# Adding the last two blocks' results of a routed layer by products with a matrix of ones and zeros, with the order of work laid out anew

## The chip, the cores and the metric

The kernel runs on one core of a Trainium2 chip. The metric is the time of one execution in device microseconds (us); the smaller the better. A profiled execution also leaves a trace, and all views quoted here are views of such a trace: the page of the profile, the chain of work that ended last, the timeline of an engine, and tables by stretches of time. PE is the engine for matrix products, DVE the vector engine, ACT the scalar engine, POOL the GpSimd engine, SP the engine that only issues transfers here.

## The reference, cut to what matters

Two layers, each of cross attention and of a feed-forward part with 8 experts, of which each token takes the best two. All data are float32.

```python
B, S, D = 4, 512, 128          # 4 sequences of 512 tokens, width 128
KV, HEADS, HD = 77, 16, 8      # context of 77 rows per sequence
E, F, TOP_K = 8, 512, 2
for layer in (0, 1):
    x = x + tanh(g_xattn[layer]) * attention(layernorm(x), context)
    xn = layernorm(x)
    w = softmax(xn @ router); keep the best two of 8 for each token
    h = gelu(einsum('td,edf->tef', xn, w1) + b1)
    y = einsum('tef,efd->ted', h, w2) + b2
    x = x + tanh(g_ffn[layer]) * sum over the two kept experts of w * y
```

The attention of layer 1 also has slopes by position and a mask. The output is `x`, of shape (4, 512, 128).

## The kernel before, in words

**Attention** works on one sequence `b` at a time, with tokens in four tiles of 128 (`NT`). `LS`, `LT`, `LU` are the layer norm (statistics on DVE, the power -1/2 on POOL, scaling on ACT, transposes on PE), `Q` the queries, `S0` to `S3` the scores whose row maxima DVE takes, `M` and `W` lower the scores by these maxima, `X0` to `X3` are the exponentials, `U0` to `U3` the weighted sums, `E`, `T`, `N`, `F` divide by the sums, project and add to `x_sb[b]`.

**Routing** (`RS` to `RX`) makes a second layer norm, the logits, the two choices and, by products with a triangle and a matrix of ones, the row of a DRAM table `xg` that each (token, choice) pair goes to. `Z0` to `Z3` send the rows: each `Z` is two indirect DMAs of 128 rows on POOL. Every such DMA has a memset on POOL ahead of it (`Scatters.send`, L416: the memset is L418, the DMA L419). A row carries the token's data, the weight of the pair and, in its last column, the row of a second table `yk` where the result belongs. Sequences 0 and 1 are group 0, sequences 2 and 3 are group 1; each group has its own `xg` and `yk`. When a group's rows are counted (`RB`, `RG`), SP loads 16 numbers, the first row of each block.

**Blocks.** Each group has 16 blocks: 7 of 256 rows and 9 of 128 rows, each of one expert. `w` loads the expert's weights (578 KB, 5 buffers) and `x` the rows (6 buffers), both on SP's queue; `t` transposes on PE and copies on DVE; `u` is the first product with the gelu on ACT; `d` the second product and, on DVE, the bias and the weight of the pair (L681, L687) and the address (L692); `y` sends the results to `yk` with one or two indirect DMAs on POOL (8 buffers `yb`).

**Combine.** `CL` loads a sequence's two results per token from `yk` (two transfers of 256 KB), `CA` adds both to `x_sb[b]` (L718: on POOL in layer 0, on DVE in layer 1) and in layer 1 sends `x_sb[b]` out (L720). A `CL` has to wait until every scatter of its group has landed.

**Order.** Nothing is scheduled by the compiler: `ORDER` is a list of such steps, written out, and every engine and every DMA queue carries out its instructions in that order. A step is written `1d15.1`: layer 1, step `d` of block 15, group 1; for attention and routing steps the last number is the sequence. `hot` is a product of the identity with itself, whose result nobody reads. The last steps of the list before are

```
1t14.1 1CL.0 1u14.1 1t15.1 1y12.1 1d14.1 1CL.1 1y13.1 1u15.1 1y14.1 1d15.1 1CA.0 1CA.1 1y15.1 1CL.2 1CL.3 1CA.2 1CA.3
```

Of the kernel before, what the change touches and what calls it, by code (L numbers as in the profile page):

```python
# [8 lines left out]
F32 = mybir.dt.float32  # L9
# [30 lines left out]
ROWS = SPARE + 2 * CAP  # L40


@with_exitstack
def flamingo_kernel(ctx: ExitStack, tc: tile.TileContext, a: dict, out: bass.AP):
# [15 lines left out]
    def bank():  # L60
        return ps_mm.tile([P, 512], F32, tag="mm", name="mm")
# [36 lines left out]
    def load_mask(b):  # L98
        t = keep.tile([P, NT * KV + S], I32, tag="mi", name="mi", bufs=2)
        nc.sync.dma_start(out=t, in_=a["masks"][b])  # L100
        msk_i[b] = t
# [499 lines left out]
    class Blocks:  # L601


        def __init__(self, routing):
            self.r, self.l, self.group = routing, routing.l, routing.group
            self.w, self.x, self.xT, self.h, self.y = {}, {}, {}, {}, {}
            self.scatters = Scatters()
# [60 lines left out]
        def down(self, i):  # L668
            n, w, h, x = self.size(i), self.w.pop(i), self.h.pop(i), self.x.pop(i)
# [19 lines left out]
            )  # L689

# [3 lines left out]

        def scatter(self, i):
            yb, to = self.y.pop(i)
            for s in range(self.size(i)):
                self.scatters.send(yks[self.l][self.group], yb[:, s, :], to[:, s : s + 1])

    class Combine:  # L700
# [14 lines left out]
        def add(self):  # L715
            x = x_sb[self.b]
            for k in range(2):
                (nc.gpsimd if self.l == 0 else nc.vector).tensor_tensor(x, x, self.y[:, k], ALU.add)  # L718
            if self.l == 1:
                (nc.scalar if self.b == B - 1 else nc.sync).dma_start(out=out[self.b].rearrange("(p t) d -> p t d", p=P), in_=x)  # L720
# [11 lines left out]
    def routing_constants():  # L732
# [25 lines left out]
        return rank, region, below, ones, upper, mark, nth, block_no, row_of, pair_at, spare  # L758
# [3 lines left out]
    fill = const.tile([P, CAP // P * PAY], F32, tag="fill", name="fill")  # L762
# [5 lines left out]
    def clear(g, q):  # L768
        xg = xgs[g]
        for e in range(4 * q, 4 * q + 4, 2):  # L770
            nc.sync.dma_start(
                out=xg[e * REGION : (e + 2) * REGION, :].rearrange("(r q) d -> r (q d)", r=2)[:, : CAP * PAY].rearrange(
                    "r (p f) -> p r f", p=P
                ),
                in_=fill.unsqueeze(1).to_broadcast([P, 2, CAP // P * PAY]),
            )
        if q == 0:
            nc.sync.dma_start(
                out=xg[UNUSED : UNUSED + 256, :].rearrange("(p r) d -> p (r d)", p=P), in_=fill[:, : 2 * PAY]
            )  # L780

# [63 lines left out]
    def part(l, name, n):  # L845
        k, i = name[0], name[1:]
        A, R = at[l][n], routings[l][n // 2]
        if i.isdigit():
            i = int(i)
            if k in "wxtudy":  # L850
                G = blocks[l][n]
                {"w": G.load_w, "x": G.load_x, "t": G.turn, "u": G.up, "d": G.down, "y": G.scatter}[k](i)
# [14 lines left out]
        vclear0 pads0 ldx0 ones0 hot1 ldwv ldctx slots hot2 0LS.0 ldo0 ldgates ldq0 vclear2 gate keys0 vclear1 ldx1  # L867
        ldx2 hot5 ones1 ldx3 0LT.0 0LS.1 ldpos ldmask1 values1 0LS.2 values0 hot0 0LU.0 fill values2 second 0Q.0 0LT.1
        0S3.0 0LT.2 hot4 0S2.0 cleara1 0S0.0 cleara0 0LU.1 ldmask0 0LU.2 0S1.0 mask1 0Q.1 0M.0 0W.0 0S3.1 0Q.2 0LS.3
        0S2.1 0X0.0 0S0.1 0X1.0 0S1.1 pads1 0U0.0 0X2.0 0M.1 0U1.0 0E0.0 clearb0 0W.1 0X3.0 routing 0U2.0 0X0.1 0U3.0  # L870
        0E1.0 0T0.0 0LT.3 0S2.2 0U0.1 0S3.2 0X1.1 0S1.2 0T1.0 0LU.3 0S0.2 0U1.1 0N.0 mask0 0M.2 0X2.1 0E0.1 0F.0 0Q.3
        0X3.1 0RS.0 0W.2 0U2.1 0RT.0 0S3.3 0U3.1 0E1.1 0S2.3 0RU.0 0T0.1 0T1.1 0RL.0 vclear3 0N.1 0RC.0 0RD.0 0X0.2
        0F.1 0RS.1 clearb1 0X1.2 0U0.2 0X2.2 0RM.0 0RN.0 0RX.0 0Z0.0 0RT.1 values3 0S0.3 0U1.2 0S1.3 0M.3 0Z1.0 0RU.1
        0RL.1 mturn0 0W.3 0X3.2 0RC.1 0U2.2 0E0.2 0X0.3 0Z2.0 0Z3.0 0RD.1 0U3.2 0E1.2 0RM.1 0T0.2 0X1.3 0T1.2 0RN.1
        0RX.1 0U0.3 0RB.1 0Z0.1 0N.2 0U1.3 0Z1.1 mturn1 0F.2 0RS.2 0Z2.1 0Z3.1 0X3.3 0X2.3 0RT.2 0RU.2 0RL.2 0RG.1
        0E0.3 0w0.0 0U2.3 0RC.2 0RD.2 0U3.3 0x0.0 0x1.0 0RM.2 0RN.2 0E1.3 0RX.2 0x2.0 0T0.3 0x3.0 0Z0.2 0Z1.2 0x4.0
        0T1.3 0N.3 0t0.0 0F.3 0w1.0 0RS.3 0w2.0 0u0.0 0Z2.2 ldq1 0RT.3 0t1.0 0d0.0 0w3.0 0u1.0 0RU.3 0t2.0 0t3.0 0u2.0
        0w4.0 0d1.0 0t4.0 0RL.3 0u3.0 0RC.3 0w5.0 0Z3.2 0RD.3 0d2.0 0x5.0 0x6.0 0x7.0 0t5.0 0u4.0 0t6.0 0y0.0 0w6.0
        0RM.3 0x8.0 0d3.0 0RN.3 0w7.0 0u5.0 0RX.3 0w8.0 0RB.3 0x9.0 0t7.0 0d4.0 0w9.0 0d5.0 0x10.0 0y1.0 0RG.3 0x11.0
        0u6.0 0t8.0 keys1 0w10.0 0y2.0 0Z0.3 0u7.0 0Z1.3 0t9.0 0d6.0 0w11.0 0u8.0 0Z2.3 0t10.0 0Z3.3 0y3.0 0d7.0 0d8.0  # L880
        0u9.0 hot3 0x12.0 0w12.0 0d9.0 0y4.0 0y5.0 0t11.0 0u10.0 0x13.0 0t12.0 0u11.0 0d10.0 0w13.0 0y6.0 0x14.0
        0w14.0 0x0.1 0w0.1 0t13.0 0u12.0 0d11.0 0x15.0 0w15.0 0x1.1 0u13.0 0t14.0 ldmask2 0y7.0 0d12.0 0t0.1 0u14.0
        0d13.0 0y8.0 0u0.1 0w1.1 0x2.1 0t15.0 0y9.0 0t1.1 0w2.1 0x3.1 0d0.1 0y10.0 0u1.1 0y11.0 0x4.1 0d14.0 0w3.1
        0x5.1 0d1.1 0y12.0 0x6.1 0t2.1 0u15.0 0y13.0 0t3.1 0d15.0 0w4.1 0x7.1 0w5.1 0y14.0 0y15.0 0u2.1 0w6.1 0u3.1
        0t4.1 0y0.1 0d2.1 0t5.1 0u4.1 0y1.1 ldmask3 0w7.1 0t6.1 0d3.1 0u5.1 0CL.0 0t7.1 0CA.0 0d4.1 0d5.1 0u6.1 0x8.1
        0u7.1 0CL.1 0w8.1 0CA.1 0x9.1 1LS.0 0w9.1 0t8.1 0w10.1 0d6.1 0u8.1 0t9.1 1LT.0 0y2.1 0x10.1 0d7.1 1LS.1 0w11.1
        0d8.1 0x11.1 0t10.1 0y3.1 1LU.0 0w12.1 0y4.1 0u9.1 ldo1 1Q.0 0y5.1 0t11.1 1S0.0 0y6.1 0u10.1 1LT.1 0w13.1
        0d9.1 0x12.1 0t12.1 1S2.0 0u11.1 0d10.1 1S1.0 1LU.1 0u12.1 0y7.1 0w14.1 0d11.1 0x13.1 1S3.0 1M.0 1Q.1 0y8.1
        0t13.1 1S0.1 0u13.1 0y9.1 0x14.1 0w15.1 0t14.1 0x15.1 0d12.1 0t15.1 1S2.1 0u14.1 1W.0 1S1.1 0d13.1 0u15.1
        0y10.1 0y11.1 1X0.0 0y12.1 0d14.1 0y13.1 0y14.1 0d15.1 1S3.1 0y15.1 1U0.0 1M.1 0CL.2 1X1.0 1X2.0 1U1.0 1W.1  # L890
        1X3.0 1E0.0 1U2.0 0CL.3 mask2 0CA.2 1X0.1 1LS.2 1U3.0 1E1.0 1X1.1 1LT.2 1U0.1 1T0.0 1X2.1 mturn2 1T1.0 1U1.1
        1LU.2 0CA.3 1LS.3 1N.0 1X3.1 1F.0 1Q.2 mask3 1RS.0 1S0.2 1RT.0 mturn3 1U2.1 1E0.1 1LT.3 1S2.2 1S1.2 1U3.1
        1S3.2 1E1.1 1RU.0 1LU.3 1M.2 1T0.1 1T1.1 1RL.0 1W.2 1N.1 1RC.0 1RD.0 1X1.2 1F.1 1X0.2 1Q.3 1RM.0 1RN.0 1RS.1
        1RX.0 1Z0.0 1RT.1 1S0.3 1U0.2 1S3.3 1RU.1 1X2.2 1RL.1 1RC.1 1Z1.0 1S2.3 1U1.2 1RD.1 1Z2.0 1X3.2 1U2.2 1RM.1
        1S1.3 1E0.2 1RN.1 1Z3.0 1U3.2 1E1.2 1RX.1 1Z0.1 1M.3 1T0.2 1T1.2 1W.3 1N.2 1X0.3 1RB.1 1F.2 1X1.3 1U0.3 1Z1.1
        1X2.3 1Z2.1 1Z3.1 1RG.1 1U1.3 1X3.3 1U2.3 1U3.3 1E0.3 1RS.2 1w0.0 1w1.0 1E1.3 1x0.0 1RT.2 1T0.3 1x1.0 1T1.3
        1N.3 1RU.2 1F.3 1t0.0 1RL.2 1u0.0 1w2.0 1RC.2 1RS.3 1RD.2 1x2.0 1x3.0 1d0.0 1t1.0 1w3.0 1y0.0 1RT.3 1w4.0
        1RM.2 1RN.2 1RX.2 1u1.0 1t2.0 1RU.3 1t3.0 1x4.0 1x5.0 1x6.0 1RL.3 1u2.0 1RC.3 1RD.3 1Z0.2 1RM.3 1t4.0 1d1.0
        1RN.3 1w5.0 1x7.0 1Z1.2 1u3.0 1w6.0 1RX.3 1t5.0 1Z2.2 1RB.3 1d2.0 1d3.0 1u4.0 1Z3.2 1x8.0 1Z0.3 1Z1.3 1Z2.3
        1x9.0 1RG.3 1d4.0 1u5.0 1d5.0 1w7.0 1t6.0 1t7.0 1u6.0 1t8.0 1w8.0 1u7.0 1w9.0 1w0.1 1Z3.3 1y1.0 1x0.1 1d6.0  # L900
        1d7.0 1u8.0 1t9.0 1u9.0 1y2.0 1y3.0 1y4.0 1x1.1 1x10.0 1d8.0 1w10.0 1x2.1 1t0.1 1t1.1 1u0.1 1w1.1 1t10.0 1y5.0
        1d0.1 1w2.1 1d9.0 1y6.0 1x3.1 1x4.1 1w3.1 1u10.0 1t2.1 1y7.0 1x11.0 1u1.1 1d1.1 1y0.1 1t3.1 1u2.1 1x5.1 1d10.0
# [100 lines left out]
```

## Time and profile before

| | us |
|---|---|
| median of 3 runs (427.59 to 429.42) | 428.34 |
| the profiled execution, its own time | 429.68 |
| its span in the trace | 427.6 |
| PE busy | 385.3 (90%) |
| POOL busy | 295.5 (69%) |
| DVE busy | 244.9 (57%) |
| ACT busy | 225.0 (53%) |

The span runs from the first to the last event of the trace; the execution's own time holds 2.1 us more. PE is the busiest engine over the whole span, but a mean says little here: attention, blocks and the end have different limits.

### The profile page before, as it was taken

To read this page: it belongs to the slowest core of one execution; us is meant where nothing else is said; L and a number is where in the kernel's file an instruction comes from. 1 tells how busy PE (TensorE), PEld (TensorE's weight loads), DVE (VectorE), ACT (ScalarE), POOL (GpSimd) and SP (SyncE) were. 2 spreads that over 40 slices of the span, in tenths; PEclk is the share of its full clock that TensorE was granted. 3 is DMA by queue.
4 is the path that set the end of the run, shared out by engine and by line. 5 is a ranking of instruction groups with operands and counts; after the bars stand their busy time and mean duration, and the time that the engine had idled before them with its cause. 6 is when DMAs were issued, how large, how long until landed. Compare 5 with 4: busy or idle time off the path is not lost.

```text
span 427.6 us, 9653 instructions
## 1 busy us (share of the span) xinstructions
PE 385.3 (90%) x3236; PEld 271.4 (63%) x3236; DVE 244.9 (57%) x931; ACT 225.0 (53%) x529; POOL 295.5 (69%) x478
## 2 busy tenths in 40 slices
PE   5999999987899999989999999999889999999850
PEld 2454545433789999987772355442669789988840
DVE  7786768864447634376774379684648233333342
ACT  2556776663374654447455965446564344435430
POOL 4743312887698989869986450987289898989860
PEclk9999999996699999999999999999989999999995
DMA  7396091112956799986514221014743776789855
GB/s 191 158 372 202 3 325 72 33 44 83 317 150 207 224 361 295 313 299 218 167 45 151 80 60 62 26 45 122 236 129 105 272 232 192 266 285 289 269 204 182
DMA packets 38977, 77.91 MB, mean 182 GB/s; under 512 B 6224, under 2 KB 22608, under 8 KB 38928
## 3 DMA queue, kind: packets, MB, share of 16 engines
q1 hardware_dynamic: 32640, 65.66, 47.9%
q0 software_dynamic: 4992, 10.30, 6.7%
q10 hardware_dynamic: 1296, 1.34, 0.9%
q8 instruction: 26, 0.43, 0.4%
q14 instruction: 23, 0.19, 0.1%
HBM read 55.47 MB, written 21.80 MB: 181 GB/s over the span
## 4 chain that ended last, share of the span: by engine, by line
PE 68%; DVE 12%; DMA 6%; POOL 5%; ACT 4%; issue 3%; SPq 0%; DVEq 0%; ACTq 0%; POOLq 0%
PE mm L673 16%; PE mm L658 15%; PE mm L353 8%; PE o L367 7%; PE mm L305 6%; POOL xg L419 3%; PE mm L279 3%; DVE mx L313 2%; PE mm L347 2%; ACT eT L359 2%; POOL apart L418 2%; PE mm L241 2%; PE mm L643 2%; PE mm L406 2%; DMA xb<-xg 1%
## 5 line engine op out<-in xcount | busy, mean ns | idle before, releaser
L664 ACT ACTIVATE h<-mm,w 128x128 f32<-128x128 f32 (+1 forms) x256 | 86.7, 415 | 99.3 <-issue 55.9
L419 POOL DMA_INDIRECT yk<-yb,to x92 | 89.6, 974 | 18.5 <-issue 12.2
L658 PE MATMUL mm<-xbT,w 128*128 128x128 f32 (+1 forms) x512 | 95.0, 331 | 6.6 <-DVE xbT L645 5.5
L673 PE MATMUL mm<-w,h 128*128 128x128 f32 x736 | 96.0, 281 | 0.7 <-ACT h L664 0.4
L673 PEld LDWEIGHTS mm<-w,h 128*128 128x128 f32 x736 | 89.2, 191 | 6.5 <-ACT h L664 3.6
L658 PEld LDWEIGHTS mm<-xbT,w 128*128 128x128 f32 x512 | 77.1, 194 | 15.0 <-DVE xbT L645 7.7
L418 POOL MEMSET apart<- 1x512 f32 x156 | 80.2, 514 | 0.1
L359 ACT ACTIVATE eT<-mm 77x512 f32<-77x512 f32 x128 | 65.4, 592 | 26.2 <-PE mm L353 25.7
L419 POOL DMA_INDIRECT xg<-rows,rows_to x64 | 62.8, 981 | 15.2 <-issue 13.0
L681 DVE TENSOR_TENSOR yb<-mm,w 128x128 f32<-128x128 f32 (+1 forms) x64 | 22.3, 348 | 67.2 <-PE mm L673 58.6
L313 DVE TENSOR_REDUCE mx<-mm 128x4 f32<-128x308 f32 x128 | 52.1, 469 | 11.5 <-PE mm L305 11.3
L353 PE MATMUL mm<-qa,kb 32*77 32x512 f32 x256 | 41.3, 617 | 0.5 <-DVE mx L313 0.5
L222 POOL TENSOR_SCALAR rstd<-mv 128x4 f32<-128x4 f32 x16 | 3.8, 236 | 54.2 <-DVE mv L220 40.9
L645 DVE COPY xbT<-mm 128x128 f32<-128x128 f32 (+1 forms) x64 | 21.7, 344 | 30.4 <-PE mm L643 30.4
L367 PE MATMUL o<-eT,vb 128*32 128x512 f32 x256 | 36.6, 631 | 0.0
L305 PE MATMUL mm<-kb,q 32*128 32x154 f32 x512 | 31.8, 322 | 0.8 <-DVE mx L313 0.5
L305 PEld LDWEIGHTS mm<-kb,q 32*128 32x128 f32 x512 | 22.6, 183 | 12.4 <-issue 3.1
L687 DVE TENSOR_TENSOR yb<-yb,xb 128x128 f32<-128x128 f32 (+1 forms) x64 | 24.1, 376 | 2.2
L643 PE MATMUL mm<-ident,xb 128*128 128x128 f32 x92 | 20.5, 281 | 1.2 <-DMA xb<-xg 1.2
L353 PEld LDWEIGHTS mm<-qa,kb 32*77 32x77 f32 x256 | 10.5, 140 | 13.4 <-issue 5.6
L223 POOL TENSOR_TENSOR rstd<-rstd,mhalf 128x4 f32<-128x4 f32 x16 | 16.7, 1044 | 1.3
L219 DVE BATCH_NORM_STATS2 st<-x 128x6 f32<-128x128 f32 x64 | 17.1, 267 | 0.2
(155 smaller groups left out, 445.6 us busy)
## 6 DMA issues: line engine op xcount, KB each, us to landing
w<-in_experts SPq DMA_DIRECT2D x64, 578.0 KB, 5.0
xg<-fill SPq DMA_DIRECT2D x8, 1040.0 KB, 6.0
xb<-xg SPq DMA_DIRECT2D x28, 130.0 KB, 3.6
y<-yk SPq DMA_DIRECT2D x14, 256.0 KB, 3.9
mt<-turns SPq DMA_DIRECT2D x4, 820.0 KB
xb<-xg SPq DMA_DIRECT2D x36, 65.0 KB, 4.4
mi<-in_masks SPq DMA_DIRECT2D x4, 410.0 KB
turns<-mb SPq DMA_DIRECT2D x8, 205.0 KB
```

Source lines behind the costliest of these rows:

```text
L305: nc.tensor.matmul(view[g][:, h], lhsT=self.q[h][rows, t * P : (t + 1) * P], rhs=kbs[l][rows, h, :, b, :], start=(l == 0), stop=(l == 0 or ...
L313: nc.vector.tensor_reduce(self.mx[:, t, :, 2 * g : 2 * g + 2], view[g], AX.X, ALU.max)
L353: nc.tensor.matmul(ps[g][:KV, :], lhsT=kbs[l][rows, h, w, b, :], rhs=self.qa[h][rows, :], start=(l == 0), stop=True,)
L359: nc.scalar.activation(self.eT[j][g][:KV, :], ps[g][:KV, :], AF.Exp)
L367: nc.tensor.matmul(self.o[a][g * 32 : (g + 1) * 32, :], lhsT=vbs[self.b][:, self.l, g, j, :], rhs=self.eT[j][g], start=(w == 0), stop=(w = ...
L418: nc.gpsimd.memset(apart, 0.0)
L419: i = nc.gpsimd.indirect_dma_start(out=to[:, :], out_offset=bass.IndirectOffsetOnAxis(ap=index, axis=0), in_=rows, in_offset=None)
L643: nc.tensor.transpose(ps[:, s * P : (s + 1) * P], x[:, s, :D], ident)
L658: nc.tensor.matmul(ps[:, g * 256 : g * 256 + n], lhsT=w[:, c * P : (c + 1) * P], rhs=xT[:, :n], start=True, stop=True,)
L664: nc.scalar.activation(h[:, c, :n], ps[:, g * 256 : g * 256 + n], AF.Gelu_apprx_tanh, bias=w[:, B1_AT + c : B1_AT + c + 1])
L673: nc.tensor.matmul(y[:, s * P : (s + 1) * P], lhsT=h[:, c, s * P : (s + 1) * P], rhs=w[:, W2_AT + c * P : W2_AT + (c + 1) * P], start=(c = ...
L687: nc.vector.tensor_tensor(yb[:, :n, :], yb[:, :n, :], x[:, :n, D : D + 1].to_broadcast([P, n, D]), ALU.mult)
```

## The change

The results of blocks 14 and 15 of layer 1, group 1, no longer go to `yk`. For each of these blocks a new step `o` (`match`) compares on DVE the token number of each row with all 1024 tokens of the group, which gives a matrix of ones and zeros `oh` (128 x 2 x 512); `y` of these blocks (`give`) multiplies `oh` with the block's results on PE (8 products of 128x128x128) and adds the two outputs of 128x512 to `x_sb[2]` and `x_sb[3]` on DVE. The output of sequences 2 and 3 is sent by block 15's `give`, no more by `CA`. Rows of `yk` that now stay unwritten are cleared once (`cleary`, one transfer of 1 MB). To make room, the buffer of zeros `fill` becomes a quarter wide enough for four rows a partition, `clear` issues four transfers instead of two for the same bytes, and the raw masks have one buffer instead of two. `ORDER` is laid out anew from end to end.

```diff
-        t = keep.tile([P, NT * KV + S], I32, tag="mi", name="mi", bufs=2)
+        t = keep.tile([P, NT * KV + S], I32, tag="mi", name="mi", bufs=1)
...
+            if self.last(i):
+                self.y[i] = yb, None
+                return
...
+        def last(self, i):
+            return self.l == 1 and self.group == 1 and i >= NBLK - LAST
+
+        def match(self, i):
+
+            v = self.x[i][:, 0, D + 1 : D + 2]
+            tok = small.tile([P, 2], F32, tag="tok", name="tok", bufs=2)
+            nc.vector.tensor_scalar(tok[:, 0:1], v, float(ROWS + SPARE + CAP), -float(CAP), ALU.is_ge, ALU.mult)
+            nc.vector.tensor_tensor(tok[:, 0:1], tok[:, 0:1], v, ALU.add)
+            nc.vector.tensor_scalar(tok[:, 1:2], tok[:, 0:1], -float(S), None, ALU.add)
+            oh = blk.tile([P, 2, S], F32, tag="oh", name="oh", bufs=1)
+            for b in range(2):
+                nc.vector.tensor_scalar(oh[:, b], token_at, tok[:, b : b + 1], None, ALU.is_equal)
+            self.oh[i] = oh
+
+        def give(self, i):
+
+            yb, _ = self.y.pop(i)
+            oh = self.oh.pop(i)
+            for b in range(2):
+                ps = bank()
+                for t in range(NT):
+                    own = slice(t * P, (t + 1) * P)
+                    nc.tensor.matmul(ps[:, own], lhsT=oh[:, b, own], rhs=yb[:, 0, :], start=True, stop=True)
+                x = x_sb[2 + b]
+                nc.vector.tensor_tensor(x, x, ps.rearrange("p (t d) -> p t d", d=D), ALU.add)
+                if i == NBLK - 1:
+                    (nc.scalar if b else nc.sync).dma_start(out=out[2 + b].rearrange("(p t) d -> p t d", p=P), in_=x)
+
         def scatter(self, i):
+            if self.last(i):
+                self.give(i)
+                return
...
-            if self.l == 1:
-                (nc.scalar if self.b == B - 1 else nc.sync).dma_start(out=out[self.b].rearrange("(p t) d -> p t d", p=P), in_=x)
+            if self.l == 1 and self.b < 2:
+                nc.sync.dma_start(out=out[self.b].rearrange("(p t) d -> p t d", p=P), in_=x)
...
+        token_at = counted("token_at", [P, S], [[1, NT], [NT, P]], base=ROWS + SPARE)
...
-    fill = const.tile([P, CAP // P * PAY], F32, tag="fill", name="fill")
+    fill = const.tile([P, 4 * PAY], F32, tag="fill", name="fill")
...
-        for e in range(4 * q, 4 * q + 4, 2):
+        for e in range(4 * q, 4 * q + 4):
...
+    def clear_results():
+
+        nc.sync.dma_start(
+            out=yks[1][1][ROWS + SPARE :, :].rearrange("(n p r) d -> p n (r d)", r=4, p=P),
+            in_=fill[:, : 4 * D].unsqueeze(1).to_broadcast([P, 2 * CAP // 512, 4 * D]),
+        )
```

Of the order, these stretches are spoken of below. The kernel's first steps, layer 0 at the first blocks, layer 1 at the first blocks, and the end, each before (-) and after (+), with steps between them left out where "..." stands:

```diff
- vclear0 pads0 ldx0 ones0 hot1 ldwv ldctx slots hot2 0LS.0 ldo0 ldgates ldq0
+ ones0 ldctx vclear2 hot2 ldx0 pads0 slots hot1 ldgates ldwv ldq0 vclear0 0LS.0
...
- 0RX.2 0x2.0 0T0.3 0x3.0 0Z0.2 0Z1.2 0x4.0 0T1.3 0N.3 0t0.0 0F.3 0w1.0 0RS.3
+ 0T0.3 0w1.0 0RN.2 0RX.2 0E1.3 0x3.0 0T1.3 hot3 0N.3 0Z0.2 0w2.0 0F.3 0x4.0 mturn0 0t0.0 0t1.0 0Z1.2 0u0.0 0t2.0 0Z2.2 0x5.0 0RS.3
...
- 1Z2.1 1Z3.1 1RG.1 ... 1RS.2 ... 1t0.0 1RL.2 1u0.0 1w2.0 1RC.2 1RS.3 1RD.2 ... 1d0.0 1t1.0 1w3.0 1y0.0 1RT.3 1w4.0 1RM.2 1RN.2 1RX.2 ... 1Z0.2
+ 1Z2.1 1RS.2 ... 1Z3.1 1RG.1 1RT.2 ... 1RL.2 ... 1RC.2 1RD.2 1RM.2 1x4.0 1F.3 1RN.2 1RX.2 1t0.0 1x5.0 1Z0.2 ... 1RS.3 ... 1u0.0 ... 1Z3.2 ... 1y0.0
...
+ 1y15.0 1t13.1 1w13.1 1y7.1 1u12.1 1x14.1 1w14.1 1CL.0 1x15.1 1o14.1 1u13.1 1y8.1 1d12.1
+ 1t14.1 1y9.1 1w15.1 1d13.1 1y10.1 1u14.1 1CL.1 1CA.0 1y11.1 1t15.1 1y12.1 1d14.1 1u15.1 1CA.1 1d15.1 1y13.1
+ 1CL.2 1y14.1 1CL.3 1o15.1 1CA.2 1CA.3 1y15.1
```

## The prediction, on record before the changed kernel ran

> **What bounds the kernel now.** First the page, slices of 10.7 us:
>
> ```profile
> PE   5999999987899999989999999999889999999850
> POOL 4743312887698989869986450987289898989860
> PEclk9999999996699999999999999999989999999995
> ```
>
> PE is close to full except at the start, around slice 9, around slice 28 and at the end. POOL is as full in the two stretches of blocks (slices 10 to 20 and 29 to 38). Of what ended the span I read the chain of waits from 400 us on; columns are start, length, what:
>
> ```profile
> 412.30 1.28 PE mm L673 x8
> ...
> 417.85 4.21 DMA y<-yk
> ...
> 423.48 0.69 DVE x L718
> ```
>
> After PE's last product (413.58) 14 us pass without PE: the last scatter, its landing, the load back, the adds, the output. The scatters before it are in POOL's timeline (start, length, what, in brackets the idle time before and what ended it):
>
> ```profile
> 402.86 0.96 POOL L419 DMA_INDIRECT yk<-yb,to  x1 [0.17 <-DVE yb L681]
> ...
> 409.44 0.96 POOL L419 DMA_INDIRECT yk<-yb,to  x1 [0.17 <-issue]
> ...
> 412.35 0.96 POOL L419 DMA_INDIRECT yk<-yb,to  x1 [1.44 <-DVE to L692]
> ...
> 414.56 1.16 POOL L419 DMA_INDIRECT yk<-yb,to  x1 [0.73 <-DVE to L692]
> ```
>
> The first is `1y15.0`; six scatters follow it. Four of them lie (409.44 - 402.86) / 4 = 1.645 us apart with 0.17 us of idle time: POOL is saturated there, and has been since 311.40 us, where layer 1's first scatter stands. So the end is set by POOL's queue, and I count from T0, the start of `1y15.0`'s scatter. Before, the end is T0 + 24.7.
>
> Last, PE at layer 0's first blocks and the granted clock there (PE's and four more busy times, PEclk, DMA share, GB/s):
>
> ```profile
> 108.00:112.00 4.00, 2.82 (x12) 2.45 (x13) 1.12 (x4) 1.87 (x2) 3.60 (x5) 0.55 0.96 264
> 112.00:116.00 4.00, 4.00 (x16) 3.36 (x16) 2.31 (x9) 1.03 (x3) 2.35 (x5) 0.60 0.99 354
> ```
>
> A pause of 1.43 us before `0N.3` (108.88) was followed by about 6.5 us at half clock.
>
> **The end, counted from T0.** The change leaves seven scatters behind `1y15.0` (`1y7.1` to `1y13.1`) instead of six, and `1CL.2` waits for the last.
> - Seven at 1.645 and the last one's 0.96: POOL is done at T0 + 12.5.
> - Landing: unknown, since the last scatter now lands while weights and `CL.1` are loaded. Bounds: 1.4 us (415.72 to the load's issue at 417.11, nothing else in flight) and 4.1 us (`1y15.0` ended at 403.82, `1CL.0` was issued at 407.96, DMA busy). I take the middle, 2.75, because part of the traffic is over by then: T0 + 15.2.
> - Loads of `CL.2` and `CL.3`: 417.47 to 422.06, 4.6: T0 + 19.8.
> - `CA.2` and `CA.3`, four adds of 0.69: T0 + 22.6. The two adds of `1y15.1` read PSUM; the nearest row is L408, 128x512 from PSUM, 0.75 each: T0 + 24.1.
> - From the last add to the end as before, 424.17 to 427.6: T0 + 27.5.
>
> [...]
>
> The other path to the same adds goes by block 15. SP's queue now holds `x15` and `w15` behind `CL.0`, which waits for `1y15.0` to land. `CL.0` is issued at T0 + 5.1, as before; two issues of it 0.9, `x15` 0.6, `w15` 0.3: T0 + 6.9. `w15` lands 5.1 later (the chain has a `w` of 5.06): T0 + 12.0. From `u15` to the end of `d15` 2.4 us (411.18 to 413.58): T0 + 14.4. `1y14.1`: 8 products, 16 rows at 0.11 (L673, 8 in 0.89): T0 + 16.2, one add 0.75: T0 + 17.0. `1o15.1`: three small operations at 0.16 and two of 128x512, between 0.24 (L801, 128x32) and 0.75 (L408); I take 0.75, the row of that width: 2.0, so T0 + 19.0. That is 0.8 us ahead of the loads: block 15, the products and the comparisons hide behind the loads, and cost what exceeds 0.8 us. `1y15.1`'s products, at half clock after PE's pause (the clock fell to 0.50 from 416 us on), take 3.5 us and lie beside `CA.2` and `CA.3` and the first add, 3.5 us.
>
> So the end after T0 is 2.8 us **longer** than before; what pays is that T0 is earlier.
>
> **T0.** Before it stand three scatters fewer than before (the two lists, counted): 3 x 1.645 = 4.9 us earlier while POOL is saturated. `d15.0` permits it: it stands 5.8 us of PE work earlier in the new list, and before it was ready at 399.9, 3 us ahead of its scatter.
>
> Upstream, four terms:
> - Start: `wk` was issued at 4.17, after `wv` had landed (the chain has 0.80 + 3.35), the transfers having eight slots. In the new list it is the seventh transfer and issues about 1.4 us earlier. ACT's norm of sequence 0 (11.77) stands behind the four `kb` that need `wk`, and needs `nmr` (10.99; 0.3 earlier, one operation of 0.3 less on the way): it can start at about 10.7. Taken: -1.1.
> - `values3` now stands ahead of `0RX.0`: four copies of 0.15, +0.6 on POOL's first `Z`.
> - `0T0.3` stands ahead of `0RX.2`: 0.36 + 0.42 on DVE, +0.8.
> - `0RS.3` made POOL wait 1.40 us at 115.39; it now stands two scatters later: -1.4.
>
> Sum -1.1. `hot3` moves from the middle of the blocks (0.9 us of PE) into the pause before `0N.3`. If the clock then stays up, PE gains up to 2.1 us at 115, but at 153 to 159 the chain goes through POOL and a landing (`yk`, 5.21 us), and PE would wait there. I take 0 and keep -2.1 for the range.
>
> Layer 1: `1RS.2` stands ahead of `1Z3.1`, and `1RX.2` ahead of `1t0.0`. The first scatter after the pause, `1Z0.2`, can start at about 308.2 (`1U3.3` ends at 299.2, then some 2.8 us to the logits' end at 302, then 5.7 us from logits to `rows_to`, as from 101.58 to 107.29 in layer 0) instead of `1y0.0` at 311.40; but 1.3 us of `1RS.3` no longer lies in the pause. Gain 0 to 1.9; PE waits for `1RN.2` before its first block, so I take 1.0.
>
> T0 = 402.86 - 4.9 - 1.1 - 1.0 = 395.9, and the span ends at 395.9 + 27.5 = 423.4, 4.2 us earlier. The profiled execution's own 429.68 becomes 425.5. The runs' median lies 1.34 below it, so I predict 428.34 - 4.2 = 424.1.
>
> **Edits costed at nothing.** `clear`: eight more issues on SP at 0.86, 6.9 us; SP stood 24.2 us waiting for the masks in those 55 us, and `xg` is first written at 75.1. If the cover failed, the first `Z` would slip by up to 6.9. `cleary`: one issue and 1 MB, 2.6 us at the 390 GB/s of full stretches; it stands at layer 0's blocks where the DMA share is 0.34 to 0.87, and the `w` behind it slip by that much within five buffers; uncovered, 2.6. One mask buffer: `ldmask3` waits for POOL's `mask2`, and `ldo1` and `x` of layer 1 stand near it on SP; needed only by `1S0.3`; uncovered about 3 (`mask` took 3.0). The early `wk1`/`wq1` and `x3` behind `turns1`: `x3` should land near 32.5 and is read at about 36; the margin is 3.5 us, and what exceeds it stops DVE's maxima. `token_at`: between 0.2 (iota 128x32) and 0.95 (memset 128x1024) on POOL, in 6.95 us of idle time before `0RS.0`. `1CA.0` and `1CA.1` (1.4 each on DVE) now stand ahead of `t15`'s copy and `d15`'s bias; they lie beside the wait for `w15`.
>
> **Rivals.**
> 1. *Given back at the end* (0.20). `w15` lands 3 us later, since 512 KB of `CL.0` and two `xb` go ahead of it (one `xb` took 5.61 us in this stretch). Then block 15 decides: T0 + 29.6, and with T0 at 397 a span of 426.6, 427.3 by the median. For it: DMA share 0.9 there. Against: the weights of block 15 were never late before.
> 2. *Slower: PE starved at layer 1's first block* (0.17). `1RN.2` now stands ahead of `1t0.0` on PE, so PE waits out the choice of experts: 5.7 + 0.7 + 0.4 us, then half clock for 6.6 us (3.3 lost), 10.1 in all against some 4 lost there now (1.4 and 0.6 of waits, clock 0.65 in 312 to 316). Everything in POOL's queue follows: T0 = 395.9 + 1.0 + 6.1 = 403.0, span 430.5, 431.2 by the median. It decides from T0 = 402.2 on. Against: `1N.3` and `1F.3`, some 2 us of PE work, stand inside that wait.
> 3. *More than forecast* (0.13). The clock stays up at 108 to 116, POOL starts 1.9 earlier and the landing takes 1.4: T0 = 392.9, span 419.0, 419.7 by the median.
>
> **How the numbers follow.** The forecast has 0.50; its own range, from the bounds above, is 419.7 to 427.5. About 0.5% (2.1 us) is what a measurement of this kernel can tell from no change: 426.2 and 430.5. Faster takes forecast and rival 3 without a little of the upper end, 0.62; same, mostly rival 1, 0.21; slower 0.17. For 8 in 10 the range goes from 417.5 to 431.0.
>
> **What would show it.** `1y15.0`'s scatter near 396 and the last scatter seven places behind it; SP's `CL.2` some 2.75 us after that one's end; DVE's last four `x` adds and two PSUM adds back to back behind the load; layer 0's clock at 108 to 116. I am wrong if `1y15.0` stands later than 402, if DVE's last adds wait for PE and not for the load, or if POOL shows pauses over 2 us between 310 and 395.

## The result, and the profile after

The changed kernel takes 427.27 us by the median of 20 runs (425.4 to 430.33), the kernel before 430.38 by 20 runs beside it. The ratio of the two is 0.9947, with a 95% interval of 0.9926 to 0.9968: faster by 0.5%, some 2.3 us. (The ratio leaves disturbed executions of both out, the medians do not.) The forecast was 424.1 us, 4.2 us faster. The sign and the range held; the size was too large.

The two profiled executions lie apart by just the forecast: 425.46 us (span 423.7) against 429.68 (427.6). That agreement is luck, as the steps show. (0.3 us of the 4.2 lie outside the span: in every run of the changed kernel its own time holds 1.7 to 1.8 us more than its span, before about 2.1. No run tells why.) First the page, slices of 10.6 us:

```profile
PE   6899999987899989999999999989899688999992
POOL 5443251898789889869886540996199898989750
PEclk9999999996999999999999999989799999999999
```

Counted from 1: PE now has a hollow at slices 32 to 34 (328 to 360 us), where it was full before. The clock has new dips at slices 27 and 29 beside the one at slice 10; the dips of before at 11, 30 and 40 are gone. The end, in the chain of waits (start, length, what):

```profile
400.91 5.30 DMA y<-yk
...
406.85 0.96 POOL yk L420
...
408.50 3.41 DMA yk<-yb,to
...
412.30 4.24 DMA y<-yk
...
417.96 0.69 DVE x L754
```

The last scatter starts at 408.50 (1.24 us long) instead of 414.56; its landing is over at 411.90, 2.2 us after its end, and the loads behind it end at 416.54. POOL's timeline from `1y15.0`, whose start is T0:

```profile
394.55 0.96 POOL L420 DMA_INDIRECT yk<-yb,to  x1 [0.17 <-issue]
396.19 0.96 POOL L420 DMA_INDIRECT yk<-yb,to  x1 [0.17 <-issue]
397.84 0.96 POOL L420 DMA_INDIRECT yk<-yb,to  x1 [0.17 <-issue]
400.71 0.96 POOL L420 DMA_INDIRECT yk<-yb,to  x1 [1.40 <-DVE to L696]
402.36 0.97 POOL L420 DMA_INDIRECT yk<-yb,to  x1 [0.17 <-issue]
404.01 1.08 POOL L420 DMA_INDIRECT yk<-yb,to  x1 [0.17 <-DVE tok L707]
406.85 0.96 POOL L420 DMA_INDIRECT yk<-yb,to  x1 [1.24 <-DVE xbT L646]
408.50 1.24 POOL L420 DMA_INDIRECT yk<-yb,to  x1 [0.17 <-issue]
```

Seven scatters follow T0, as said, but two of them stand behind pauses of 1.40 and 1.24 us: POOL is no longer saturated there. The names in the brackets are DVE's steps of a block, and these stand behind PE's products: POOL waits for PE. The addresses (`to`) of block 12, before and after, show that PE is no earlier at this block than before:

```profile
406.19 0.15 DVE L692 TENSOR_TENSOR to<-xb,spare 128x1 int32<-128x1 f32 x1
```

```profile
406.42 0.15 DVE L696 TENSOR_TENSOR to<-xb,spare 128x1 int32<-128x1 f32 x1
```

They are ready at 406.34 and 406.57. Last, layer 0's first blocks (PE and four more busy times, PEclk, DMA share, GB/s):

```profile
108.00:112.00 4.00, 2.29 (x17) 1.84 (x17) 1.30 (x4) 1.87 (x2) 3.66 (x6) 1.00 0.95 274
112.00:116.00 4.00, 4.00 (x21) 3.54 (x22) 1.92 (x9) 2.60 (x7) 3.49 (x6) 1.00 1.00 315
```

The clock is 1.00 where it was 0.55 and 0.60.

### The profile page after: what moved, and what is told of

The parts are those of the page before. It is cut to its first block, busy times and chain, and to the rows that moved or that the text cites. A ratio compares the mean times of both kernels' runs of the same rounds, so it can differ in the third digit from the quotient of the medians.

```text
span 423.7 us, 9735 instructions
## 1 busy us (share of the span) xinstructions
PE 386.9 (91%) x3268; PEld 274.4 (65%) x3268; DVE 248.6 (59%) x943; ACT 225.1 (53%) x529; POOL 294.2 (69%) x475
## 4 chain that ended last, share of the span: by engine, by line
PE 54%; POOL 17%; DMA 11%; DVE 7%; issue 6%; ACT 3%; DVEq 0%; SPq 0%; POOLq 0%; ACTq 0%
PE mm L659 10%; PE mm L674 10%; POOL xg L420 9%; PE mm L354 7%; PE o L368 6%; PE mm L306 6%; POOL apart L419 5%; PE mm L280 3%; DMA xg<-rows,rows_to 2%; DMA w<-in_experts 2%; DMA y<-yk 2%; DMA yk<-yb,to 2%; PE mm L242 2%; POOL yk L420 2%; PE mm L348 2%
## 5 line engine op out<-in xcount | busy, mean ns | idle before, releaser
L659 PE MATMUL mm<-xbT,w 128*128 128x128 f32 (+1 forms) x512 | 93.8, 328 | 9.1 <-DMA w<-in_experts 5.6
L420 POOL DMA_INDIRECT yk<-yb,to x90 | 87.9, 976 | 17.5 <-issue 12.9
L674 PE MATMUL mm<-w,h 128*128 128x128 f32 x736 | 94.6, 279 | 0.5 <-ACT h L665 0.2
L360 ACT ACTIVATE eT<-mm 77x512 f32<-77x512 f32 x128 | 65.5, 592 | 27.5 <-PE mm L354 27.1
L419 POOL MEMSET apart<- 1x512 f32 x154 | 79.2, 514 | 0.1
L354 PE MATMUL mm<-qa,kb 32*77 32x512 f32 x256 | 42.4, 623 | 0.1
L688 DVE TENSOR_TENSOR yb<-yb,xb 128x128 f32<-128x128 f32 (+1 forms) x64 | 22.5, 352 | 2.2
```

The lines of the kernel that those rows point to most:

```text
L354: nc.tensor.matmul(ps[g][:KV, :], lhsT=kbs[l][rows, h, w, b, :], rhs=self.qa[h][rows, :], start=(l == 0), stop=True,)
L360: nc.scalar.activation(self.eT[j][g][:KV, :], ps[g][:KV, :], AF.Exp)
L419: nc.gpsimd.memset(apart, 0.0)
L420: i = nc.gpsimd.indirect_dma_start(out=to[:, :], out_offset=bass.IndirectOffsetOnAxis(ap=index, axis=0), in_=rows, in_offset=None)
L659: nc.tensor.matmul(ps[:, g * 256 : g * 256 + n], lhsT=w[:, c * P : (c + 1) * P], rhs=xT[:, :n], start=True, stop=True,)
L674: nc.tensor.matmul(y[:, s * P : (s + 1) * P], lhsT=h[:, c, s * P : (s + 1) * P], rhs=w[:, W2_AT + c * P : W2_AT + (c + 1) * P], start=(c = ...
```

## The experiments: the two halves of the change

Ratios are to the kernel before on the same chip, with 95% intervals. First the changed kernel again, then each half alone.

> The changed kernel once more, unaltered, for a second profiled execution and for its place beside the parts that run on the same chip. Theory A (the gain is real and about as large as between the medians: -3 us): ratio to before 0.992 to 0.995, and the second profile shows the last scatter of y13.1 near 408.5 to 410 and the same two pauses of POOL (1.2 and 1.1 us) before it. Rival B (the first profile was an early one, and its T0 of 394.55 is not typical): in the second profile 1y15.0 starts 1.5 to 2 us later, at 396 to 396.5, with the steps behind it unchanged, and the execution takes about 427.3.

Measured: 0.9955 (0.9921 to 0.999), median 427.66 against 429.77. The second profile has span 424.6, T0 at 394.73, the two pauses again and the last scatter at 409.06. Theory A holds; T0 is not what was untypical.

```diff
# e2: the order of before, with
+ 0d5.0 cleary
- 1t14.1 1CL.0 1u14.1 1t15.1 1y12.1 1d14.1 1CL.1 1y13.1 1u15.1 1y14.1 1d15.1 1CA.0 1CA.1 1y15.1 1CL.2 1CL.3 1CA.2 1CA.3
+ 1t14.1 1CL.0 1o14.1 1u14.1 1t15.1 1y12.1 1d14.1 1CL.1 1CA.0 1u15.1 1CA.1 1d15.1 1y13.1 1CL.2 1y14.1 1CL.3 1o15.1 1CA.2 1CA.3 1y15.1
```

> The order of before, with the last two blocks' results given by products (clear of the rows, comparisons, products, outputs behind them); only ldmask0 and ldmask3 are moved behind mask1 and mask2, for the one mask buffer. Theory A (end and order add up, some half each): y13.1's scatter stays at 409.4, CL.2 is issued some 2.5 us after its end, 412.9, loads until 417.5, four adds to 420.3, two adds from PSUM to 422, end 425.5: 2.1 us faster, ratio 0.993 to 0.997. Rival B (the end gives all of it): ratio 0.990 to 0.993, the order alone 1.000. Rival C (the end gives nothing, since comparisons and products replace the landing): ratio 0.998 to 1.002.

(`ldmask0` and `ldmask3` moved besides, as said there.) Measured: 1.0005 (0.996 to 1.005). The end alone gives nothing that can be measured: rival C by its number, though not by its reason. The last scatter starts at 410.55, 4 us earlier than before, but the chain of waits of this kernel shows what came then:

```profile
415.96 0.15 SPq L756
...
416.66 4.19 DMA y<-yk
...
422.27 0.69 DVE x L754
```

That scatter ended at 411.52. The other half of these loads, on ACT, was issued at 415.78, so the landing took 4.3 us; on SP they stood behind the output of sequence 1 (L756) to 416.28. In these microseconds `CL.0` and `CL.1` are loaded, 1 MB issued at 409.44 to 411.21.

```diff
# e3: the order of the changed kernel, with
- LAST = 2
+ LAST = 0
- 1d15.1 1y13.1 1CL.2 1y14.1 1CL.3 1o15.1 1CA.2 1CA.3 1y15.1
+ 1d15.1 1y13.1 1y14.1 1y15.1 1CL.2 1CL.3 1CA.2 1CA.3
```

> The order of the changed kernel, with LAST = 0: blocks 14 and 15 are scattered again behind y13.1, no comparisons, no products, no clear of the result rows. Theory A: POOL's saturated stretch in layer 1 starts some 3.4 us earlier as in the changed kernel, T0 at 394.5 to 396, but d15 ends only at about 411.5, so the last scatter stands near 412.3 (before 414.56) and the end follows 12 us behind its end as before: 425 to 425.5, 2.3 us faster, ratio 0.993 to 0.997. Rival B (order gives nothing): ratio 0.999 to 1.001. Rival C (order gives all of it): 0.990 to 0.993.

(The `o` steps and `cleary` are left out too, and `CA` sends all four outputs again.) Measured: 0.9974 (0.9942 to 1.0006). T0 stands at 395.03, as expected, but the last scatter starts at 415.65, not 412.3, 1.1 us later than before the change, and the wait ahead of it (1.66 us) is for DVE's `to` of block 15. With 7.8 us gained at T0, POOL's queue was empty before PE had block 15. So each half removes one of two limits: the order alone leaves the last scatters waiting for PE, the end alone leaves the landing behind the loads of `CL.0` and `CL.1`. The intervals are too wide to show by times alone that the halves together give more than their sum; the traces show the two limits.

## The experiments: the end

```diff
# e5: 1y15.0 behind 1y9.1; both e5 and e6:
- 1CL.0 1x15.1 ... 1w15.1
+ 1x15.1 ... 1w15.1 1CL.0
```

> The changed kernel with 1y15.0 three places later in POOL's queue (behind 1y9.1, six products' scatters... the place that it has before the change: four scatters of this list behind it), and CL.0 behind w15.1 on SP. Theory A (the end pays only because 1y15.0 stands early: CL.0 and CL.1, 1 MB, are then loaded before y13.1 lands; in the run of the end alone they were issued at 409.4 to 411.2 and y13.1's landing took 4.3 us where the changed kernel shows 2.2): CL.0 is issued at about 405, the landing of y13.1 takes 3.5 to 4.5 us, CL.2 is issued about 2 us later, and the kernel is 1.5 to 2.5 us slower than the changed one. Rival B (the landing does not depend on these loads): the landing stays at 2.2 to 2.5 us and the time within 0.7 us of the changed kernel's.

> The changed kernel with CL.0's two loads behind x15 and w15 on SP's queue, nothing else. Theory A (SP waits for a buffer of w there anyway, and block 15 has slack): x15 and w15 are issued about 1 us earlier, POOL's pauses before y9.1 and y12.1 stay within 0.3 us, time within 0.7 us of the changed kernel. Rival B (rival 1 of the prediction: the loads of CL.0 hold block 15 and through it the end): the end comes 1 us or more earlier.

Measured on one chip: e5 1.0006 (0.9971 to 1.0041), e6 0.9966 (0.9929 to 1.0003); medians 430.33 and 428.86. In e5 `CL.0` was issued only at 408.65, later than expected, and the landing of `1y13.1` took 3.7 us (its scatter ended at 411.76, ACT's loads were issued at 415.50); in e6 2.7 us (end 412.07, ACT's loads at 414.72). The direction is theory A's; 1.5 us between the medians is at its lower edge, and the intervals overlap. In e6 nothing was won, but the edit moved little: `w15` was issued at T0 + 7.5 instead of T0 + 7.7, because SP waited for a buffer there anyway. `CL.0` ahead of `x15` and `w15` thus costs next to nothing, and rival 1's mechanism is not what took the rest.

## The experiments: layer 1's first blocks

```diff
# e9
- 1F.3 1RN.2 1RX.2 1t0.0 ... 1u0.0
+ 1F.3 1t0.0 1u0.0 1RN.2 1RX.2
```

> The changed kernel with 1t0.0 and 1u0.0 ahead of 1RN.2 on PE, as they stand before the change: the place of rival 2. Theory A (layer 1's first scatters wait for the choice of experts, and PE's pause there costs nothing that POOL does not lose anyway): 1Z0.2 starts 0.5 to 2.5 us later than 306.4, because 1.8 us of u0 or a wait for its weights stand before the places; the end is 0 to 2 us later. Rival B (rival 2, PE starved there, is where part of the forecast was lost): granted clock stays up in 302 to 309 and the kernel is 1 to 2 us faster than the changed one.

Measured: 1.0081 (1.0051 to 1.011), the largest effect of all: some 5 us slower than the changed kernel, beyond what theory A allowed (1Z0.2 was to slip by 2.5 us at most). PE waits in `u0` for its input, with the places of sequence 2 (L522) behind it; then POOL's first scatter after the pause. Two views of e9, PE's timeline and POOL's:

```profile
306.43 1.99 PE L659 MATMUL mm<-xbT,w 128*128 128x256 f32 x8 [2.25 <-DVE xbT L646]
308.26 0.30 PE L522 MATMUL mm<-m,upper 128*128 128x32 f32 x2
```

```profile
310.30 0.98 POOL L420 DMA_INDIRECT xg<-rows,rows_to  x1 [10.07 <-issue]
```

In the changed kernel that scatter stands at 306.51. The 3.8 us are found again at T0 (398.42) and at the last scatter (412.31): a late start of layer 1 reaches the end undiminished (with both pauses of POOL again, 1.27 and 1.25 us, so PE is late by as much). So rival 2's place is where the new order gains; the change from `1t0.0` to `1RN.2` ahead is a cause of the gain, not a loss.

Where PE loses its lead, the waits of the changed kernel between 332 and 362 us tell (us in total, times, longest). Two of SP's between 300 and 350 tell what stood ahead of the loads:

```profile
PE mm L659 <- DMA w<-in_experts: 5.3, 2, 3.3
PE mm L644 <- DMA xb<-xg: 1.5, 1, 1.5
PE mm L659 <- DVE xbT L646: 0.2, 1, 0.2
```

```profile
SPq L597 <- DVE begins L596: 8.6, 1, 8.6
...
SPq L632 <- DMA xg<-rows,rows_to: 5.7, 1, 5.7
```

Before the change PE waited 2.1 us in the same stretch, and not for `w`. Two kernels were meant to win this back.

```diff
# e7
- 1w0.1 1u7.0 ... 1Z3.3 1x0.1 1u8.0 1y1.0 1t0.1 1d8.0 1t9.0 1y2.0 1x1.1 1x10.0 1u0.1 1u9.0 1d0.1 1w1.1 1t10.0 1x11.0 1w10.0
+ 1u7.0 ... 1w9.0 1w0.1 ... 1Z3.3 1x10.0 1w10.0 1u8.0 1y1.0 1x11.0 1x0.1 1d8.0 1t9.0 1y2.0 1u9.0 1t10.0 1t0.1 1d9.0 1x1.1 1u0.1 1u10.0 1d0.1 1w1.1
# e17
- w = blk.tile([P, WROW], F32, tag="w", name="w", bufs=5)
+ w = blk.tile([P, WROW], F32, tag="w", name="w", bufs=6)
```

> The changed kernel with 1x0.1 (which waits for the landing of Z3.3) and 1w0.1 later on SP, so that x10, w10 and x11 of group 0 go ahead of that wait, and 1t0.1, 1u0.1 behind u9 and t10 on PE. Theory A (PE's lead is lost between 332 and 360, where it waits 3.3 us for w, 1.5 for xb, 2.0 for w, and SP stands 6 us at x0.1; that lead is what POOL waits for before y9.1 and y12.1): PE's waits for loads in 332 to 360 fall from 6.8 to about 3 us, the two pauses of POOL (1.2 and 1.1) shrink below 0.5, y13.1 stands 1.5 to 2.3 us earlier and the kernel is 1.5 to 2 us faster than the changed one. Rival B (there the transfers themselves are the bound, and the order on SP only shifts who waits): PE's waits keep their sum within 1 us, and the time stays within 0.7 us.

> The changed kernel with six buffers of expert weights instead of five (room for it comes from scaling the output bias in place); the order is untouched. Theory A (the term of the forecast that failed is POOL saturated to its end: PE comes late to d9 and d12 because it stood 6.8 us at loads between 332 and 360, 5.3 of it at w, whose issue waits for a buffer): PE's waits for w there fall below 2.5 us, the scatters from 1y7.1 to 1y13.1 take 11 to 12 us instead of 12.3, the kernel is 1.5 to 2.5 us faster than the changed one, ratio to before 0.988 to 0.991. Rival B (the transfers themselves or the landing of Z3.3 hold PE): waits for w within 1.5 us of 5.3, ratio 0.993 to 0.996.

Measured: e7 0.9919 (0.9889 to 0.9949), e17 0.993 (0.9899 to 0.9961). In e7 PE's waits in 332 to 362 sum to 6.6 us instead of 7.0: only the names changed, although the last scatter stands 1.1 us earlier (407.42) and the time is perhaps 0.3% better. In e17 the waits for `w` there are as long as in the changed kernel:

```profile
PE mm L659 <- DMA w<-in_experts: 5.6, 2, 3.4
```

For the first and longer wait both theories named the wrong holder. Neither a buffer nor `x0.1` keeps `w7` of group 0 back, but L597, ahead of both on SP: `1RG.3`, the reading of group 1's block table into SP's registers, stands in the order ahead of `1w7.0`, waits 8.6 us for `begins`, and only then are the next four loads of weights issued (333.04 to 336.55). That is read from the trace; a kernel with `1RG.3` behind `1w9.0` was not run. The second wait (2.0 us, at 358) is not a wait for `w` any more in e7, but waits for rows (`xb`, and `xbT` made from them) stand in its place.

## The experiments: the clock

> The changed kernel with hot3 back at its old place behind 0u9.0, so that nothing runs on PE in the pause before 0N.3. Theory A (the clock falls again but POOL sets the time there): clock 0.5 to 0.6 at 108 to 116, PE some 2 us later at 0t0.0, and 0y0.0's scatter the same to 0.5 us later because POOL is saturated from 0Z0.2 on; time against the changed kernel 0 to +0.5 us. Rival B: the 1.4 us that POOL gains between 0Z0.2 and 0Z0.3 come from the clock, and the kernel is 1.5 us slower than the changed one.

Measured: 0.9961 (0.9925 to 0.9996), as the changed kernel. The pause before `0N.3` was 1.47 us long with nothing in it, and the clock stayed up all the same; windows of e4:

```profile
108.00:112.00 4.00, 2.38 (x17) 1.94 (x18) 1.30 (x4) 1.87 (x2) 3.66 (x6) 1.00 0.96 260
112.00:116.00 4.00, 3.73 (x18) 3.08 (x19) 1.88 (x10) 2.22 (x6) 3.49 (x6) 1.00 1.00 342
```

So the clock did not need `hot3` here: 1.43 us were followed by half clock before the change (0.55 and 0.60 in these windows), 1.47 us in e4 were not. The end of this profile is the nearest to the forecast's. Its T0 is 394.55, and POOL's last two scatters are

```profile
405.38 0.96 POOL L420 DMA_INDIRECT yk<-yb,to  x1 [0.93 <-DVE xbT L646]
407.02 1.24 POOL L420 DMA_INDIRECT yk<-yb,to  x1 [0.17 <-issue]
```

With one pause instead of two the span is 422.1, T0 + 27.55: the 27.5 of the forecast. T0 is that of the first profile; what differs ahead of the end is PE, which begins the block behind its last long wait at 356.98 instead of 358.23, and the last scatter stands 1.48 us earlier (407.02). These two profiles are the best evidence that PE sets the place of the last scatter.

Products into PE's pauses were then tried, because the time of the 32 runs of the changed kernel goes with their mean granted clock (correlation -0.61; 1.7 us for 0.01 of clock).

```diff
# e8 (and e15): the changed kernel with; e13 the last two only, e14 the first two only
- 0RT.2 ... 1W.3 ... 1F.3
+ hot6 hot7 0RT.2 ... hot8 1W.3 ... hot9 1F.3
# e11 (and e16): the kernel before with
- 0RT.2 ... 0N.3 ... 1RN.2
+ hot6 hot7 0RT.2 ... hot8 0N.3 ... hot9 1RN.2
# e10: e7 and e8 together; e18: e10 and e17 together; e12: e10 with
- hot6 hot7 0RT.2 ... 0RL.2
+ hot6 hot7 hot6 0RT.2 ... hot6 0RL.2
```

> The changed kernel with four more products of ones matrices that nothing reads (as hot3) put into PE's pauses: two before 0RT.2 (pause 2.76 us, clock 0.5 in 98 to 104), one before 1W.3 (pause 1.98, clock 0.5 in 282 to 285 in some executions), one before 1F.3 (pauses 0.42, 0.68 and 0.34, clock 0.5 in 302 to 309). Theory A (the pauses bring the half clock, and in front of 1Z0.2 it lies on the path: logits of sequence 2 to its places): granted clock 1.00 in those stretches, 1Z3.1 at 292.5 instead of 294.0, 1Z0.2 at 304 to 305 instead of 306.4, POOL's whole stretch and the end 1 to 2 us earlier, and a smaller spread. Rival B (PE's half clock is off the path, POOL and the choice of experts decide): clock up, but 1Z0.2 within 0.5 us of 306.4 and the time within 0.7 us of the changed kernel's.

> The later x0.1 and w0.1 together with the four products in PE's pauses, on the changed kernel. Theory A (two separate losses: PE's lead given back in front of Z3.3's landing, some 1 us by the timed runs, and the half clock, some 3 us): they add, 423 to 424.5 median, ratio to before 0.982 to 0.988. Rival B (both buy the same lead of PE): no better than the four products alone, 0.986 to 0.989, with PE's waits for loads between 332 and 360 as long as there.

> The kernel before with four such products in its own pauses: two before 0RT.2 (pause 2.49), one before 0N.3 (1.43), one before 1RN.2 (1.43). Theory A (the pauses that the new order makes longer, 2.0 us before 1W.3 and 0.4 + 0.7 + 0.3 around 1F.3, took back part of what the change gives; the order of before had only 0.8 us at the first of them and one half-clock stretch of 3.4 us in layer 1): before gains little, 0.995 to 0.999, and the changed kernel with its pauses filled stands 0.9% to 1.1% below this one, as forecast for the change. Rival B (half clock costs either order the same): before gains as much as the changed kernel did, 0.990 to 0.993, and the distance stays at 0.5%.

> The kernel of the later x0.1 with the four products, and two more at layer 0: a third before 0RT.2 (1.0 us of pause was left there and the clock still fell at 99 in the profiled execution) and one before 0RL.2 (0.68). Theory A (layer 0's half clock at 98 to 106 delays 0Z0.2 and with it POOL's first full stretch): clock 1.00 at 98 to 106, 0Z0.2 at 106.5 instead of 107.7 to 109, and 0.5 to 1 us less than with four. Rival B (POOL recovers it in its idle time at 226 to 268 anyway): no difference beyond 0.5 us.

> The changed kernel with only the two products in layer 1's pauses (one before 1W.3, one before 1F.3). Theory A (the half clock ahead of 1Z0.2 is what took back part of the forecast): most of what four products gave, ratio to before 0.986 to 0.990. Rival B (layer 0's half clock at 98 to 106 is the costly one): 0.993 to 0.996, as the changed kernel.

> The changed kernel with only the two products before 0RT.2 in layer 0. Theory A: 0.993 to 0.996, as the changed kernel, because what layer 0 gains is given back in the pause before 1W.3, where DVE decides. Rival B: most of what four gave, 0.986 to 0.990.

> All four products on the changed kernel once more, beside its halves and beside the kernel before with its own four, on one chip. Expected from the first time: 0.984 to 0.990. Theory A of the kernel before with products: 0.9% to 1.1% below that kernel here. Rival: 0.5%.

> The kernel before with four products in its own pauses, on the same chip as the three others. Expected from the first time: 0.994 to 0.998.

> Six buffers of weights, the later x0.1 and w0.1, and the four products in PE's pauses, on the changed kernel. Theory A (PE's lead decides the end): they add in part, ratio to before 0.982 to 0.987. Rival B (POOL's queue bounds what PE can win): 0.988 to 0.992, as with the four products alone.

| kernel | ratio to before | 95% |
|---|---|---|
| e8, four products | 0.9872 | 0.9828 to 0.9916 |
| e15, the same again | 0.992 | 0.9892 to 0.9948 |
| e13, layer 1's two | 0.9917 | 0.9881 to 0.9952 |
| e14, layer 0's two | 0.9931 | 0.9904 to 0.9959 |
| e10, with the later x0.1 | 0.9912 | 0.9882 to 0.9942 |
| e12, with two more | 0.9925 | 0.9893 to 0.9957 |
| e18, with six buffers too | 0.9932 | 0.9908 to 0.9957 |
| e11, before with four | 0.9959 | 0.9937 to 0.9981 |
| e16, the same again | 0.996 | 0.994 to 0.998 |

The products help both kernels: before by 0.4%, twice; the changed one by 0.3% to 0.8%, by its ratios to before on different chips. On one chip the two filled kernels (e15, e16) stand at 0.992 and 0.996, 0.4% apart, not 0.9% to 1.1%: theory A of e11 falls, and half clock behind the pauses that were filled does not account for the missing part of the forecast. How the products help is not shown: `1Z0.2` stands at 307.52 in e8 and 305.87 in e15, not at 304 to 305 as theory A had it. Which layer's pauses count, e13 and e14 do not tell. Nothing adds to the four products: e10, e12 and e18 are no faster, and e10 and e18 lie above the ranges of both their theories. In e12 all three stretches have the full clock:

```profile
96.00:108.00 12.00, 10.03 (x53) 5.06 (x52) 8.40 (x43) 5.21 (x12) 9.29 (x14) 1.00 0.16 37
276.00:288.00 12.00, 10.80 (x135) 5.32 (x134) 9.84 (x37) 4.20 (x9) 10.64 (x16) 1.00 0.14 45
300.00:312.00 12.00, 9.62 (x61) 7.63 (x59) 8.19 (x39) 4.28 (x8) 4.50 (x9) 1.00 0.90 281
```

(the changed kernel has 0.72, 0.86 and 0.72 there), and still this span is 426.7: its POOL starts layer 1 at 307.97, 1.5 us later than the changed kernel's.

One pause was filled in none of these kernels, the longest: PE's wait for `w7`, 2.9 to 3.7 us in all 16 profiles with the new order or an edit of it. The four profiles with the old order have no wait over 1.05 us in this stretch (326 to 364). In 12 of the 16 the clock fell behind it: the eight products there take 1.13 us in the first profile and in e7, 2.04 or 2.05 in e1, e8, e9, e10, e17 and e18. Two of them, the first profile and e1:

```profile
338.23 1.13 PE L659 MATMUL mm<-xbT,w 128*128 128x128 f32 x8 [3.28 <-DMA w<-in_experts]
```

```profile
338.08 2.04 PE L659 MATMUL mm<-xbT,w 128*128 128x128 f32 x8 [3.27 <-DMA w<-in_experts]
```

So the first profile, like e4's, is one of the four that escaped. What this half clock costs was not measured. The fastest version by the runs is the changed kernel with the four products: 424.88 and 427.06 by the medians, against 430.64 and 430.85 of the kernel before beside it.

## Why the prediction was right or wrong

**The end, counted from T0: the step that failed.** "Seven at 1.645 ... POOL is done at T0 + 12.5" took POOL as saturated to its last scatter. It is done at T0 + 15.2 in the first profile and 15.6 in the second (409.06 + 1.24 - 394.73), 13.7 in e4 and 16.2 in e6: 2.7 us more on the mean of the four, most of it in pauses that wait for PE. The queue has three scatters fewer and runs 3.4 us earlier, but PE had block 12 ready at 406.57, against 406.34 before. That PE is this late because it waited 7.0 us between 332 and 362, where it waited 2.1 before, is argued from the traces: no run took these waits away. The prediction asked whether PE permits the earlier queue for `d15.0` alone, not for the seven blocks behind it. Its own view of before already had POOL waiting 1.44 and 0.73 us for `to` at the end. And its list of signs ("I am wrong if ... POOL shows pauses over 2 us between 310 and 395") placed the pauses ahead of T0, not behind it.

- Landing 2.75: 2.2 in the first profile, 2.1 in e1, 2.2 in e4, 2.7 in e6. The middle between the bounds was fair, and the upper bound of 4.1 is real (4.3 in e2). At the lower, 1.4, sequence 0's output (256 KB, issued at 415.64) was in flight, not nothing.
- Loads of `CL.2` and `CL.3` 4.6: 4.6 (411.92 to 416.54).
- Adds: four `x` adds and two from PSUM back to back behind the load, as said; one of the four ran before the load was over, and the PSUM pair took 1.28 instead of 1.5: together the adds end 3.3 us behind the load instead of 4.3. From the last add (419.85) to the end 3.85 instead of 3.4.
- Block 15's path: the comparisons end at T0 + 20.8 instead of 19.0, but the loads too are later (T0 + 22.0), so it stays hidden, by 1.2 us instead of 0.8. The two comparisons of 128x512 took 0.87 together instead of 1.5, and `1y15.1`'s products 2.02 at full clock instead of 3.5.

In sum T0 + 29.15 against 27.5; 29.5 on the mean of the four profiles.

**T0: right to 1.0 us on the mean, with its parts mis-sized.** Forecast 395.9, measured 394.55, 394.73, 394.55, 395.88 and, in e3, 395.03. Three scatters fewer gave 4.9, as counted. Upstream and layer 1 gave 3.4 instead of 2.1, by POOL's scatters one by one (earlier is minus): +0.3 at the first of layer 0 (forecast -0.5), -1.9 in the long run of that layer (-1.1), -2.2 at its end, -3.1 at the first of layer 1, -3.4 from `1Z0.3` on. The gain at layer 1's start was the uncertain term; by e9 what is lost there reaches the end whole.

- Start, -1.1: before, eight transfers were issued from 0.80 to 2.21 and the next two, `wk` among them, only at 3.97 and 4.17; now `wk` is issued at 2.70. Its products do start 0.7 us earlier (7.58 against 8.31; 0.4 on the means of all profiles), but the first scatter comes at 75.7 on the mean of 16 profiles with this start, against 74.6 in four with the old one. The term is wrong in sign there, and most of it is absorbed before 1Z0.2, which stands at 306.0 to 307.1 in the eight profiles with the same steps ahead of it, whose first scatters lie 1.9 us apart.
- `hot3`: taken 0, measured 0 (e4).
- The edits costed at nothing show no cost of their own in the chain; `CL.0` ahead of `w15` was tested (e6).

**From the profile to the median.** The forecast of 424.1 took 4.2 us from a median of three runs, 428.34. Over 17 to 35 runs each the kernel before has medians of 429.3 to 430.85: about 2 of the 3.2 us that the median misses are that base. The rest is the gain itself: 3.1 us between the medians and 2.3 by the ratio, instead of 4.2. The steps explain a part of it. On the mean of the four profiles T0 came 1.0 us earlier than forecast (394.9) and the end was 2.0 longer (29.5), so the span was 424.4, 1.0 longer than the 423.4 forecast. The profiles are also shorter than a typical execution: the first was the second fastest of its 20 runs, while the profiled one before stood 0.7 below its median. In a typical execution the span is 425.6 (427.27 less 1.7). What makes it some 1 to 2 us longer than these profiles stays open. The half clock behind the wait for `w7` goes with it in the profiles (423.7 and 422.1 us without it, 424.6 and 427.3 with it), but no run took it away; the products in the other pauses helped both kernels about alike.

**The rivals.** 1 (given back at the end): its numbers are the measured ones (T0 + 29.6 and 427.3 us), its mechanism is not: `w15` was issued at T0 + 7.7, block 15 stayed hidden behind the loads, and e6 is no faster. What lengthened the end is PE's lateness at blocks 9 and 12, which no rival named; that the numbers fit is luck. 2: refuted by e9, which is its opposite and slower. 3: no; T0 was 394.55 and not 392.9, and the landing not 1.4.

## What to carry to other kernels

When a change takes work off a saturated queue, count again from that point which engine feeds it: the next bound is as near as the slack there. Before, block 13's address was ready at 408.56, 0.9 us ahead of its scatter at 409.44, and the forecast moved this scatter 2.0 us forward. Look at what waits ahead of the loads on an issuing queue: here the reading of a table waited 8.6 us, the next four loads of weights were issued only from 333.04 to 336.55, and neither a sixth buffer nor another order of the loads behind it took PE's wait away (3.4 us in e17, 3.2 in e7). And where runs spread over 1%, take the base from many runs before a forecast of half a per cent.

## What the runs showed of the hardware

Pauses of PE between 1.4 and 2.0 us were followed by half clock in some executions and not in others, at the same place: 1.43 us at 108 us before the change were (granted clock 0.50 from 109 to 115), 1.47 us in e4 were not (1.00 from 108 to 116); 1.98 us before `1W.3` were in the first profile (0.50 from 282 to 285), 1.98 in e4 were not (1.00 from 276 to 288). Of longer ones, too, only some were: 3.28 us ahead of `w7` in the first profile and 3.43 in e4 left the clock full, 3.27 in e1 did not. Stretches at half clock lasted 3.4 us (the first profile at 282, e9 at 284), 6.8 (before the change at 98, the first profile at 302) and 10.2 (e9 at 97), by the granted clock microsecond by microsecond.

The landing of the last scatter (64 KB) took 1.4 us before the change, with the 256 KB of sequence 0's output beside it (issued at 415.64). With the 1 MB of `CL.0` and `CL.1` issued until 6 us ahead of the scatter's end it took 2.2 (changed kernel) and 2.7 (e6), until 1.4 us ahead 3.7 (e5), and until 0.3 us ahead 4.3 (e2).

The products of `wk`, 7.5 us in, take 1.27 us in some executions and 2.39 in others; the changed kernel's first profile, and e12's:

```profile
7.58 1.27 PE L179 MATMUL mm<-ctxT,wk 128*128 128x308 f32 x4 [2.37 <-DMA x<-in_x]
```

```profile
7.51 2.39 PE L179 MATMUL mm<-ctxT,wk 128*128 128x308 f32 x4 [2.29 <-DMA wk<-in_wk]
```

The first scatter stands 1.23 us later in the second (76.64 against 75.41). The two do not always go together: in e15 the products take 1.97 us, and the first scatter stands at 75.40.
